# Second product's weights loaded and summed ahead of the last gates, the last gates spread by SyncE's queue, residuals and identity in rooms of their own

## The chip, the cores and the metric

The kernel runs on one core of one Trainium2 chip. The metric is the device time of one execution in microseconds, as a median over runs. The profile is that of one execution, and its times are counted from the start of its span. The engines are TensorE (PE, with its weight loads as PEld), VectorE (DVE), ScalarE (ACT), GpSimd (POOL) and SyncE (SP, which here only issues DMAs).

## What is computed

The input x has 64 sequences of 64 channels of length 1024. A state-space convolution is taken along the length, masked by each sequence's length. Its result, 4096 tokens of 1024 values, goes through a mixture of 64 low-rank experts: scores, the best 16 with softmax gates, one product into rank space, the gates, and one product back. The result is added to x.

```python
def _L0_ffn_ref(x, A, B, Wr):
    ...
    scores = xf @ Wr.T
    top_vals, top_idx = jax.lax.top_k(scores, TOPK)
    gates = jax.nn.softmax(top_vals, axis=-1)
    G = jnp.zeros((N, K), xf.dtype).at[jnp.arange(N)[:, None], top_idx].set(gates)
    h = jnp.einsum('nd,krd->nkr', xf, A)
    out = jnp.einsum('nkr,kdr->nd', h * G[:, :, None], B)
    return (out * SCALING).reshape(*prefix, -1)
x = x + _L0_ffn_ref(_L0_cond_ref(x, itok_B_8_3872, L0_cond_log_dt, L0_cond_C, L0_cond_log_A_real, L0_cond_A_imag, L0_cond_D), L0_ffn_A, L0_ffn_B, L0_ffn_Wr)
```

All of it is in float32. The two einsums are products of 1024 x 1024 weights (A and B with their experts and ranks laid in one row) with the 4096 tokens.

## The kernel before

The channels are taken in eight groups of eight (HG), 512 tokens each. For a group, conv() makes y, gates() makes the scores on PE (psh, psc) and the softmax of the best 16 on DVE (ex), and spread_gates() transposes ex on PE with the identity (pg), stores it to gt_dram from ACT's queue and loads it back with every row repeated for 16 partitions. These eight loads of 256 KB into four gx tiles are issued by POOL (G.dma_start, L694).

Both products use a scheme of seven smaller products in place of eight (Strassen's, in Winograd's form), with sums of weight quarters and of right-hand quarters. In the first product, first() and seven() run it for a group in two halves, j = 0 and j = 2, with the products in the order 1, 6, 2, 7, 5, 4, 3; products 1 and 2 share a PSUM bank (c11), 5 and 3 another (c12). The pool ps_f has four banks. DVE takes the results out of them: u2, u3, c22 (the tile h_p, L317) and two more adds into u3 and u2 (h_u). finish() then multiplies the four quarters by the gates into one tile, hg: DVE the first quarter (b11, L721), straight from the bank c11, and POOL the other three (L715). POOL stores hg[0:3] to hg_dram, DVE makes four sums of the quarters (t1, b12, t2, t4, in sums()), and POOL stores hg[3:7] (L718). The pool hp of hg has one buffer, so each half waits for the stores of the half before it.

Around the groups, the convolution of the next group is woven into the first product of the present one, so that PE has work all the time. At the last group, 7, there is no next convolution.

The second product needs the weights of B: quarters() loads them in eight pieces of 512 KB on SP's queue (L163) into the tiles wb (s3, a22, a11, a12), factors() adds four sums of four pieces each on DVE (add_by_vector, L212), and second_level() makes, for each of the seven products, another four sums (L760), since second() runs the seven-product scheme a second time inside each of them. Their tiles lie in the pool wpb on the right side of the on-chip memory, which is opened after right.close(), that is, over the constants, the x tiles and the tables of the convolution. The constants include the identity and the tile two, both read by gates() and spread_gates().

second() runs 28 rounds, four pairs of groups (sg) by seven products n in the order 1, 6, 7, 2, 5, 4, 3. A round has seven products of its own, 1, 6, 7, 2, 5, 4, 3 again, of eight matmul instructions each in the trace, into banks named s. The right-hand tiles of a round come by SP from hg_dram (r, b_room or qy, 2 x 512 KB, loaded four rounds ahead) and get four sums on DVE (second_sums(), L777). What a round gives is added into acc_a, b_room and the output tiles o, partly on DVE from the banks (L306, L317), partly on POOL from on-chip memory (L799). The o tiles begin as the residual x, loaded by SP in fours (residuals()) into a pool op of twelve tiles, and are stored by SP. The pool op is opened after left.close(), so its tiles lie over gp, tq and hp.

Most instructions are ordered by a scheduler from the order of the program and its own costs; where the code says tc.keep_in_program_order(), an instruction keeps its place among its engine's others. Each engine works off its instructions in order. A DMA waits on the queue of the engine that issues it, and with it whatever that engine issues later.

Of the kernel before, what the change touches and what calls it, by code (L numbers as in the profile page):

```python
# [37 lines left out]
F32 = mybir.dt.float32  # L38
I32 = mybir.dt.int32
AF = mybir.ActivationFunctionType  # L40
ALU = mybir.AluOpType
# [3 lines left out]
P = 128  # L45
# [47 lines left out]
def body(ctx: ExitStack, tc, x, xo, lens, par, dvec, at, bm, wt, cst, out):  # L93
# [7 lines left out]
    def pool(stack, name, bufs, side, **kw):  # L101
        return stack.enter_context(tc.tile_pool(name=name, bufs=bufs, side=side, **kw))
# [9 lines left out]
    fp = pool(ctx, "fp", 2, "left")  # L112
    gp = pool(left, "gp", 1, "left")
    tq = pool(left, "tq", 1, "left")
    const = pool(right, "const", 1, "right")
    xp = pool(right, "xp", 4, "right")
    tp = pool(right, "tp", 1, "right")
# [6 lines left out]

    par_sb = const.tile([P, 5, NP], F32, tag="par", name="par_sb")
    nc.sync.dma_start(par_sb, par)
    cst_sb = const.tile([P, NW + P + 2 + NBLK], F32, tag="cst", name="cst_sb")
    nc.scalar.dma_start(cst_sb, cst)
    lens_sb = prep.tile([P, NB], I32, tag="lens", name="lens_sb")
    d_sb = const.tile([P, NH], F32, tag="dvec", name="d_sb")  # L130
# [3 lines left out]
    ident = cst_sb[:, NW : NW + P]  # L134
    identsel = cst_sb[:, NW : NW + P + 2]
    feat = cst_sb[:, NW + P + 2 :]
    two = const.tile([P, NE], F32, tag="two", name="two")

    krows = dram.tile([NH, KROW], F32, tag="krows", name="krows")

# [539 lines left out]
    def spread_gates(g, ex, spread):  # L680

        pg = ps_k.tile([NE, TOK], F32, tag="pk", name=f"pg_{g}")
        for t in range(NTT):
            tc.keep_in_program_order(nc.tensor.transpose(pg[:, t * P : (t + 1) * P], ex[:, t, :], ident))
        gt = gp.tile([NE, TOK], F32, tag="gt", name=f"gt_{g}")
        nc.scalar.copy(gt, pg)
        nc.scalar.dma_start(gt_dram[g], gt)
        n = P // RANK
        for j in range(0, KH, 2):
            for m in range(2):  # L690
                gx = gxp.tile([P, 2, TOK], F32, tag="gx", name=f"gx_{g}_{j}_{m}")
                for ii in range(2):
                    c = m * KH + j + ii
                    G.dma_start(  # L694
                        gx[:, ii, :],
                        gt_dram[g, c * n : (c + 1) * n, :].unsqueeze(1).to_broadcast([n, RANK, TOK]),
                    )
                spread[m, j] = gx


# [3 lines left out]
    def first(g, y, spread):  # L704

        rf = right_factors(y.rearrange("p k s h b -> p k s (h b)"), f"ty{g}_")

        def finish(j, c11, u2, u3, c12, p4, c22):
            hg = hp.tile([P, 7, 2, HT], F32, tag="hg", name=f"hg_{g}_{j}")

            def gate(m, s):
                return spread[m, j][:, :, s * HT : (s + 1) * HT]

            def gt_(o, a, b, op):
                G.tensor_tensor(out=o, in0=a, in1=b, op=op)  # L715

            def store(a, b):
                nc.gpsimd.dma_start(hg_dram[g, :, a:b, j : j + 2, :], hg[:, a:b])  # L718

            b11, b21, b22, t4, t1, t2, b12 = (hg[:, n] for n in range(7))  # L720
            i = V.tensor_tensor(out=b11, in0=c11, in1=gate(0, 0), op=ALU.mult)  # L721
            if g == 0:
                tc.keep_in_program_order(i)
            gt_(b22, c22, gate(1, 1), ALU.mult)
            tt(u3, p4, u3, ALU.subtract)
            gt_(b21, u3, gate(1, 0), ALU.mult)
            tt(u2, c12, u2, ALU.add)
            gt_(b12, u2, gate(0, 1), ALU.mult)
            store(0, 3)

            def sums():
                tt(t1, b11, b12, ALU.subtract)
                tt(b12, b22, b12, ALU.subtract)
                tt(t2, b22, t1, ALU.add)
                tt(t4, b21, t2, ALU.subtract)
                store(3, 7)

            unsummed.append(sums)

        for j in range(0, KH, 2):  # L740
            for n, _ in enumerate(seven(wa, rf, j, f"h{g}", finish)):
                if n == 1:
                    sum_factors()
                yield
# [3 lines left out]
    def sum_factors():  # L748
        while unsummed:
            unsummed.pop()()  # L750
# [32 lines left out]
    def second(places, rooms, loaded, next_loaded, made, second_level_of, spare, pools):  # L783
# [2 lines left out]

        op, ps, A, B = pools
        todo = [(sg, n) for sg in range(NG // 2) for n in (1, 6, 7, 2, 5, 4, 3)]
        outs = {}

        def residuals(sg, m, s):
            for a in range(2):
                for gg in range(2):
                    o = op.tile([P, 2, HT], F32, tag="o", name=f"o_{sg}_{m}{s}{a}{gg}")
                    queued(o.rearrange("p i t -> p (i t)"), xo[2 * sg + gg, m, s, a])
                    outs[m, s, a, gg] = o

# [96 lines left out]
        for q, (sg, n) in enumerate(todo):  # L894
            if q + 1 < len(todo):
                steps = second_sums(r_of.pop(q + 1), *rooms(q + 1))
            else:
                steps = iter(())

            def ahead_step():  # L900
                next(later, None)
                try:
                    next(steps)
                except StopIteration as e:
                    if e.value is not None:
                        sums[q + 1] = e.value

            right_ = sums.pop(q)
            left_ = made[n]
            early, late = now  # L910
            later = second_level_of(todo[q + 3][1]) if q + 3 < 7 else iter(())

            def product(i, bank=None, more=False):
                first = bank is None
                if first:
                    banks, t = (ps, "ps") if more else (ps_f, "pf")
                    bank = banks.tile([P, 2, HT], F32, tag=t, name=f"s{sg}_{n}_{i}")
                for ii in range(2):
                    for k in range(2):
                        nc.tensor.matmul(  # L920
                            bank[:, ii, :], lhsT=left_[i - 1][:, k, ii * P : (ii + 1) * P],
                            rhs=right_[i - 1][:, k, :],
                            start=(first and ii == 0 and k == 0),
                            stop=(ii == 1 and k == 1 and not more),
                            skip_group_check=True,
                        )
                return bank

            def new(t, i):
                return fp.tile([P, 2, HT], F32, tag=t, name=f"{t}{i}_{sg}_{n}")  # L930

            c11 = product(1, more=True)
            p1 = new("p", 1)
            nc.scalar.copy(p1, c11)  # L934
            p6 = product(6)
            v2 = new("u2", 2)
            tt(v2, p1, p6, ALU.subtract)
            early((0, 1), v2)
            ahead_step()
            p7 = product(7)  # L940
            v3 = new("u3", 3)
            tt(v3, p7, v2, ALU.add)
            early((1, 1), v3)
            early((1, 0), v3)
            product(2, c11)
            if q == 0:
                sum_factors()
            late((0, 0), c11, None)
            ahead_step()
            c12 = product(5, more=True)  # L950
            late((1, 1), c12, v3)
            ahead_step()
            p4 = product(4)
            late((1, 0), p4, v3)
            ahead_step()
            product(3, c12)
            late((0, 1), c12, v2)
            ahead_step()
            if q + 1 < len(todo):
                ahead, *now = parts_of(*todo[q + 1])  # L960
                ahead()
            if n in behind:
                residuals(sg, *behind[n])
            elif n == 4 and sg + 1 < NG // 2:
                residuals(sg + 1, 0, 0)
            if q + 4 < len(todo):
                r_of[q + 4] = places(q + 4)
                load_factor(*todo[q + 4], r_of[q + 4])
# [18 lines left out]
    for g in range(NG):  # L987
        ex = gates(g, y)
        spread = {}
        if products is not None:  # L990
            for _ in steps:
                pass
            if g + 1 == NG:

                ahead(products, 13 - done[0])
                spread_gates(g, ex, spread)
            for _ in products:
                pass
# [16 lines left out]
        for n in conv(g + 1, steps, got):  # L1015
            ahead(products, 1 if n is None else n)
        y = got.pop()
    right.close()
    wpb = pool(ctx, "wpb", 1, "right")
    sums = factors(*(factor(wpb, "wb", t) for t in ("s4", "s2", "s1")),  # L1020
                   *quarters(wpb, bm, "wb", nc.sync), add_by_vector, wb)
    made, spare = {}, {}
    room_of = {7: "a11", 2: "s2", 5: "s1", 4: "a22", 3: "s4"}

# [33 lines left out]
    n = 0  # L1058
    for _ in products:
        n += 1  # L1060
        if 4 <= n <= 9:
            ahead(sums, 3)
        if n == 9:
            es = [second_level_of(i, part(ey, k * NE2, 3, 2, L // 4)) for k, i in enumerate((1, 6))]
            es.append(second_level_of(7))
        if n >= 9:
            ahead(es[(n - 9) // 2], 3)
        if n == 10:
            loaded = tuple(gxp.tile([P, KH, HT], F32, tag="gx", name=f"r0_{gg}") for gg in range(2))
            load_factor(0, 1, loaded)  # L1070
# [13 lines left out]
        return pool(ctx, name, bufs, "left")  # L1084

    tp2 = lpool("tp2", 1)
    op = lpool("op", 12)
    qy = in_y("qy")
    A = four(wp.tile([P, KH, L // 2], F32, tag="a12", name="acc_a").rearrange("p k t -> p (k t)"))

# [51 lines left out]
```

## Time and profile before

| | us |
|---|---|
| median of 3 runs (1021.19 to 1022.26) | 1021.33 |
| the profiled execution | 1021.93 |
| its span, first to last instruction | 1020.2 |
| PE busy | 989.2 |
| PE weight loads busy (beside PE) | 740.6 |
| DVE busy | 718.6 |
| POOL busy | 336.2 |
| ACT busy | 165.9 |

The granted PE clock is 0.992 of full speed over the span. The convolution and the first product fill the span to about 668 us, and the second product the rest. A matmul of 128 x 256 in float32 appears as two instructions. In a line of the timeline the columns are start, duration, engine, line of the kernel, operation, output tile, input tiles, shape, count, and in brackets how long the engine was idle before and what ended it. In a line of the stretches the columns are the stretch, its length, the busy time of PE, PEld, DVE, ACT and POOL with their counts, the granted clock, the DMA share and GB/s.

### The profile page before, as it was taken

Reading aid. Unit: us, or ns where it says so; the run is one execution under the profiler, and the core shown is the slowest. Engines: PE = TensorE matmul, PEld = TensorE weight load, DVE = VectorE, ACT = ScalarE, POOL = GpSimd, SP = SyncE. Lnnn points to the kernel's source line nnn. Section 1 sums busy time; section 2 is a strip of 40 time slices with the busy share of each in tenths; the row PEclk is TensorE's granted clock in tenths of the full one; section 3 lists DMA queues with packets and bytes.
Section 4 is the critical chain, followed back from the end, with each engine's and each line's share of the span. In section 5 each row is a group of like instructions: output and inputs, shape, how many; then the busy total and the mean of one; then the engine's idle time right before and its main releaser. Section 6 shows DMA issues by size and latency. Waiting matters only on the chain.

```text
span 1020.2 us, 12148 instructions
## 1 busy us (share of the span) xinstructions
PE 989.2 (97%) x4416; PEld 740.6 (73%) x4416; DVE 718.6 (70%) x1672; ACT 165.9 (16%) x339; POOL 336.2 (33%) x286
## 2 busy tenths in 40 slices
PE   7999999999999999999999996998999999999998
PEld 2466656686686686686686585886888888888887
DVE  6887788587586587577567552988975785686674
ACT  5435041131131131131101000000000000000000
POOL 0012023023023023122122131226663764555565
PEclk9999999999999999999999998998999999999999
DMA  7213316316315315315314128455466268357432
GB/s 268 64 59 118 107 51 188 131 40 152 135 49 150 134 52 150 135 51 150 135 53 129 73 90 235 155 195 187 152 222 225 80 213 285 93 202 261 127 122 103
DMA packets 66253, 140.87 MB, mean 138 GB/s; under 512 B 9938, under 2 KB 18450, under 8 KB 66194
## 3 DMA queue, kind: packets, MB, share of 16 engines
q1 hardware_dynamic: 48288, 92.44, 27.0%
q0 software_dynamic: 16896, 46.18, 14.8%
q10 hardware_dynamic: 1010, 1.48, 0.6%
q8 instruction: 35, 0.57, 0.2%
q14 instruction: 24, 0.20, 0.1%
HBM read 92.79 MB, written 47.25 MB: 137 GB/s over the span
## 4 chain that ended last, share of the span: by engine, by line
PE 88%; DVE 5%; DMA 4%; issue 2%; POOL 0%; SPq 0%; ACT 0%; DVEq 0%; POOLq 0%; ACTq 0%
PE h L501 33%; PE s L920 31%; PE pc L580 6%; PE pc L586 5%; PE pu L554 5%; PE psh L639 3%; PE sum L189 2%; DMA hg_dram<-hg 2%; DMA gx<-gt_dram 1%; DVE t L777 1%; PE pb L276 1%; DMA waa<-in_at 1%; PE psc L648 1%; PE pb L278 1%; DVE e L760 1%
## 5 line engine op out<-in xcount | busy, mean ns | idle before, releaser
L317 DVE SCALAR_TENSOR_TENSOR s<-s,turn 128x64 f32<-128x64 f32 (+1 forms) x576 | 146.0, 302 | 36.7 <-ACT s L559 30.2
L501 PE MATMUL h<-y,was 128*128 128x256 f32 x512 | 119.7, 386 | 10.7 <-DVE h_p L317 10.7
L501 PE MATMUL h<-y,waa 128*128 128x256 f32 x512 | 122.7, 384 | 0.0
L501 PEld LDWEIGHTS h<-y,was 128*128 128x128 f32 x512 | 97.3, 193 | 31.5 <-DVE h_p L317 11.1
L501 PE MATMUL h<-ty,was 128*128 128x256 f32 x512 | 116.4, 380 | 0.0
L501 PEld LDWEIGHTS h<-y,waa 128*128 128x128 f32 x512 | 93.7, 190 | 27.0 <-issue 15.4
L501 PEld LDWEIGHTS h<-ty,was 128*128 128x128 f32 x512 | 96.6, 190 | 16.7 <-issue 3.9
L715 POOL TENSOR_TENSOR hg<-h_p,gx 128x512 f32<-128x512 f32 x16 | 27.3, 1706 | 227.0 <-DVE h_p L317 223.7
L715 POOL TENSOR_TENSOR hg<-h_u,gx 128x512 f32<-128x512 f32 x32 | 49.2, 1537 | 134.3 <-DVE h_u L306 134.1
L694 POOL DMA_DIRECT2D gx<-gt_dram x64 | 38.4, 624 | 101.9 <-DMA gt_dram<-gt 92.2
L934 ACT COPY p<-s 128x512 f32<-128x512 f32 x28 | 16.4, 587 | 321.5 <-PE s L920 299.6
L592 DVE TENSOR_TENSOR y<-pc,mask 128x512 f32<-128x512 f32 x64 | 42.4, 684 | 37.0 <-PE pc L586 37.0
L799 POOL TENSOR_TENSOR o<-o,acc_a 128x512 f32<-128x512 f32 x32 | 48.7, 1540 | 50.1 <-ACT acc_a L817 21.5
L580 PE MATMUL pc<-x,toep 128*128 128x512 f32 x128 | 62.0, 607 | 0.0
L306 DVE TENSOR_TENSOR hg<-hg 128x512 f32<-128x512 f32 x64 | 42.8, 688 | 26.9 <-POOL hg L715 26.0
L501 PE MATMUL h<-ty,waa 128*128 128x256 f32 x256 | 58.8, 382 | 0.0
L559 ACT COPY s<-pu 128x448 f32<-128x448 f32 x64 | 34.0, 532 | 140.8 <-PE pu L554 140.4
L586 PE MATMUL pc<-s,w 64*128 64x448 f32 x256 | 56.8, 562 | 0.0
L501 PEld LDWEIGHTS h<-ty,waa 128*128 128x128 f32 x256 | 47.9, 190 | 10.7 <-issue 4.6
L554 PE MATMUL pu<-x,bt 128*64 128x448 f32 x256 | 55.5, 553 | 0.0
L799 POOL TENSOR_TENSOR o<-o,b_room 128x512 f32<-128x512 f32 x32 | 50.0, 1581 | 9.8 <-DVE b_room L306 9.8
L306 DVE TENSOR_TENSOR o<-o,s 128x512 f32<-128x512 f32 x52 | 35.4, 681 | 23.6 <-PE s L920 17.9
(225 smaller groups left out, 1632.7 us busy)
## 6 DMA issues: line engine op xcount, KB each, us to landing
x<-in_x SPq DMA_DIRECT2D x32, 512.0 KB, 5.4
gx<-gt_dram POOLq DMA_DIRECT2D x64, 256.0 KB, 6.8
hg_dram<-hg POOLq DMA_DIRECT2D x16, 1024.0 KB, 6.0
o<-in_xo SPq DMA_DIRECT2D x64, 256.0 KB, 4.5
out<-o SPq DMA_DIRECT2D x64, 256.0 KB, 2.0
qy<-hg_dram SPq DMA_DIRECT2D x28, 512.0 KB, 3.6
r<-hg_dram SPq DMA_DIRECT2D x26, 512.0 KB, 6.6
hg_dram<-hg POOLq DMA_DIRECT2D x16, 768.0 KB, 4.4
```

The lines of the kernel that those rows point to most:

```text
L306: V.tensor_tensor(out=o, in0=a, in1=b, op=o_)
L317: V.scalar_tensor_tensor(out=o, in0=a, scalar=s, in1=b, op0=o1, op1=o2)
L501: nc.tensor.matmul(bank[:, ii, :], lhsT=fac[n - 1][:, k, (j + ii) * P : (j + ii + 1) * P], rhs=rf[n - 1][:, k, :], start=(first and ii == ...
L554: nc.tensor.matmul(pu[hh * NS : (hh + 1) * NS, :], lhsT=bt[:, i, (1 - c) * P + hh * NS : (1 - c) * P + (hh + 1) * NS], rhs=xt[:, hh, : NCH ...
L559: nc.scalar.copy(s[:, c], pu.rearrange("p (k b) -> p k b", b=NB))
L580: nc.tensor.matmul(pc, lhsT=toep[:, 2 * i + hh, :], rhs=xt[:, hh, :], start=True, stop=False)
L586: nc.tensor.matmul(pcs[hh][:, NB:], lhsT=w[o : o + NS, c, i, 1:], rhs=s[o : o + NS, c].rearrange("p k b -> p (k b)"), start=False, stop=(c ...
L592: marks["y"] = V.tensor_tensor(out=y[:, :, :, 2 * i + hh, :], in0=pcs[hh].rearrange("p (k s b) -> p k s b", s=NS2, b=HB), in1=mask.rearran ...
L694: G.dma_start(gx[:, ii, :], gt_dram[g, c * n : (c + 1) * n, :].unsqueeze(1).to_broadcast([n, RANK, TOK]),)
L715: G.tensor_tensor(out=o, in0=a, in1=b, op=op)
L799: tc.keep_in_program_order(G.tensor_tensor(out=o, in0=a, in1=b, op=op_))
L920: nc.tensor.matmul(bank[:, ii, :], lhsT=left_[i - 1][:, k, ii * P : (ii + 1) * P], rhs=right_[i - 1][:, k, :], start=(first and ii == 0 an ...
```

## The change

Four things are done. The identity and the tile two get a pool of their own (ids), so that the rest of the right side can be closed without waiting for the last gate transposes; the pool wpb is opened, and the weight quarters are loaded, before the last group's gates are spread. The last group's gates are loaded by SP's queue in place of POOL's, in program order. In the last group the first gate multiply (b11) is put behind the three that POOL makes, and kept there; the sums of the weights and the second-level sums are asked for earlier among the last group's products, with one more second-level set (n = 2) before the second product begins. The residuals get three pools of four tiles in place of one of twelve, and in the first round of second() the waiting sums of hg are made ahead of product 2.

```diff
@@ body
+    ids = pool(ctx, "ids", 1, "right")
     const = pool(right, "const", 1, "right")
...
-    cst_sb = const.tile([P, NW + P + 2 + NBLK], F32, tag="cst", name="cst_sb")
+    cst_sb = ids.tile([P, NW + P + 2 + NBLK], F32, tag="cst", name="cst_sb")
...
-    two = const.tile([P, NE], F32, tag="two", name="two")
+    two = ids.tile([P, NE], F32, tag="two", name="two")
@@ spread_gates
+        queue = nc.sync if g + 1 == NG else G
...
-                    G.dma_start(
+                    i = queue.dma_start(
                         gx[:, ii, :],
                         gt_dram[g, c * n : (c + 1) * n, :].unsqueeze(1).to_broadcast([n, RANK, TOK]),
                     )
+                    if queue is nc.sync:
+                        tc.keep_in_program_order(i)
@@ first / finish
-            i = V.tensor_tensor(out=b11, in0=c11, in1=gate(0, 0), op=ALU.mult)
-            if g == 0:
-                tc.keep_in_program_order(i)
+            def first_quarter():
+                i = V.tensor_tensor(out=b11, in0=c11, in1=gate(0, 0), op=ALU.mult)
+                if g in (0, NG - 1):
+                    tc.keep_in_program_order(i)
+
+            last_group = g + 1 == NG
+            if not last_group:
+                first_quarter()
             gt_(b22, c22, gate(1, 1), ALU.mult)
             tt(u3, p4, u3, ALU.subtract)
             gt_(b21, u3, gate(1, 0), ALU.mult)
             tt(u2, c12, u2, ALU.add)
             gt_(b12, u2, gate(0, 1), ALU.mult)
+            if last_group:
+                first_quarter()
             store(0, 3)
@@ second
-        outs = {}
+        outs, loads = {}, [0]
 
         def residuals(sg, m, s):
+            room = op[loads[0] % len(op)]
+            loads[0] += 1
...
-                    o = op.tile([P, 2, HT], F32, tag="o", name=f"o_{sg}_{m}{s}{a}{gg}")
+                    o = room.tile([P, 2, HT], F32, tag="o", name=f"o_{sg}_{m}{s}{a}{gg}")
...
-            product(2, c11)
             if q == 0:
                 sum_factors()
+            product(2, c11)
@@ body, the last group
             if g + 1 == NG:
-
+                right.close()
+                wpb = pool(ctx, "wpb", 1, "right")
+                wb_quarters = quarters(wpb, bm, "wb", nc.sync)
                 ahead(products, 13 - done[0])
                 spread_gates(g, ex, spread)
...
-    right.close()
-    wpb = pool(ctx, "wpb", 1, "right")
     sums = factors(*(factor(wpb, "wb", t) for t in ("s4", "s2", "s1")),
-                   *quarters(wpb, bm, "wb", nc.sync), add_by_vector, wb)
+                   *wb_quarters, add_by_vector, wb)
...
-        if 4 <= n <= 9:
-            ahead(sums, 3)
-        if n == 9:
-            es = [second_level_of(i, part(ey, k * NE2, 3, 2, L // 4)) for k, i in enumerate((1, 6))]
-            es.append(second_level_of(7))
-        if n >= 9:
-            ahead(es[(n - 9) // 2], 3)
+        if n <= 4:
+            ahead(sums, 5)
+        if n in (5, 6):
+            i = (1, 6)[n - 5]
+            ahead(second_level_of(i, part(ey, (n - 5) * NE2, 3, 2, L // 4)), 5)
+        if n in (9, 11):
+            ahead(second_level_of((7, 2)[(n - 9) // 2]), 5)
...
-    op = lpool("op", 12)
+    op = [lpool(f"op{i}", 4) for i in range(3)]
```

## The prediction, made before the changed kernel ran

> **What bounds the kernel now.** I read the page's forty slices first, then who TensorE (PE) waited for, then the timeline around each wait, then the stretches.
>
> ```profile
> PE   7999999999999999999999996998999999999998
> ...
> PEclk9999999999999999999999998998999999999999
> ```
>
> PE is busy almost everywhere; the chain of waits gives it 88% of the span. Two places are open: near 612 to 637 us and near 688 to 714 us. So only what closes PE's gaps there counts. The waits name them (engine and line, what it waited for, total us, times, longest):
>
> ```profile
> PE h L501 <- DVE h_p L317: 10.7, 1, 10.7
> PE s L920 <- DVE acc_a L306: 4.3, 1, 4.3
> PE s L920 <- DVE acc_a L317: 1.8, 1, 1.8
> ```
>
> The first is one wait in group 7, the last group of the first product. Its timeline (start, us, engine, line, what; idle before):
>
> ```profile
> 603.43 0.37 SPq L163 DMA_DIRECT2D wbs<-in_bm  x1
> ...
> 609.58 3.62 POOL L694 DMA_DIRECT2D gx<-gt_dram x6 [1.02 <-DMA gt_dram<-gt]
> ...
> 621.02 0.81 POOL L718 DMA_DIRECT2D hg_dram<-hg  x1 [2.13 <-DMA gx<-gt_dram]
> 623.64 3.43 PEld L501 LDWEIGHTS h<-ty,waa 128*128 128x128 f32 x16
> 623.85 3.62 PE L501 MATMUL h<-ty,waa 128*128 128x256 f32 x16
> 634.42 0.69 DVE L721 TENSOR_TENSOR hg<-h,gx 128x512 f32<-128x512 f32 x1 [16.67 <-DMA hg_dram<-hg]
> ...
> 637.43 0.68 DVE L317 SCALAR_TENSOR_TENSOR h_p<-h_u,h 128x512 f32<-128x512 f32 x1
> ...
> 638.16 2.07 PE L501 MATMUL h<-y,was 128*128 128x256 f32 x4 [10.69 <-DVE h_p L317]
> ```
>
> The hg tile has one buffer. VectorE (DVE) stands in order at the first gate multiply of group 7 (L721) until group 6's store of that tile has landed; h_p, for which PE waits, is four adds behind it. The store was issued at 621.02 and landed 13.2 us later (other stores: median 5.6). It was late twice over: POOL issued it behind eight gate loads, and it then shared the DMA engines with them and with the 4.2 MB of weights. The stretches show that load piled up while the time before it was empty (last columns: PE clock, DMA share, GB/s):
>
> ```profile
> 595.00:600.00 5.00, 5.00 (x25) 4.41 (x24) 2.81 (x8) 0.42 (x1) 0.00 (x0) 1.00 0.00 0
> ...
> 606.00:610.00 4.00, 4.00 (x20) 3.54 (x19) 1.03 (x2) 0.00 (x0) 2.68 (x3) 1.00 1.00 348
> ...
> 625.00:630.00 5.00, 2.47 (x12) 1.83 (x10) 0.00 (x0) 0.00 (x0) 0.00 (x0) 1.00 1.05 224
> ```
>
> The second place is different: DVE itself is full (11.38 of 12 us between 692 and 704).
>
> ```profile
> 701.07 3.78 PE L920 MATMUL s<-b_room,ey 128*128 128x256 f32 x8 [4.34 <-DVE acc_a L306]
> ...
> 704.64 3.85 PE L920 MATMUL s<-qy,wbs 128*128 128x256 f32 x12
> ```
>
> **What PE loses.** A product of the second stage, eight matmuls, starts every 1.73 us (0.2155 each); sixteen of the first take 3.45. First place: 10.69 idle, and the sixteen after it take 638.16 to 643.60, 5.44, so 1.99 of slow clock: 12.7. Second place: 1.76; 4.34, then 701.07 to 708.33 for twenty matmuls, 7.26 against 4.31, so 2.95; 0.24 at 724: 9.3. Cross-check: 28 rounds of 7 products are 28 x 12.1 = 339, and PE runs from 667.8 to 1016.2, 348.4. So 22.0 can be had at most.
>
> **What the Trainium skill says.** "TensorE: Matmul & The Clock Gate", Part 1, has the clock halve after an idle window of about 3.4 us and recover after such a window of work. The trace agrees: 10.7 and 4.3 us idle are followed by 1.99 and 2.95 lost, the 1.8 us idle by nothing. "SBUF — State Buffer", Who interferes with whom: a DVE instruction with two SBUF inputs and a GpSimd one that reads SBUF exclude each other. Here an SBUF add takes 0.68 alone and 1.75 beside POOL, while adds with a PSUM input stay at 0.68. "DMA: Bandwidth & Descriptors", Queues, rings and completion order: the engines take packets from the queues in turn, so a small store suffers from another queue's backlog; the 13.2 us agree.
>
> **The change, part by part.** The order of the built instructions tells what the diff leaves open: PE's order is the same but for three matmuls late on, ACT's is the same, and POOL loses the eight gate issues.
>
> *Weights earlier.* With identity and two elsewhere, the first weight load waits for group 7's score matmuls (psh, last at 588.8) instead of the gate transposes (pg, 603.3). So 4.2 MB start at 588.9. The same eight loads at the kernel's start ran at 260 to 400 GB/s; about 13 us, done near 602, in the empty stretch. They sit on SP's queue, with nothing urgent behind. Cost nothing.
>
> *Gates by SP.* The gate store to DRAM is still issued at 604.0, now on an empty DMA, and lands in 2.2 us (the quickest landing in that tile's view) to 5.3 (this one). SP then issues eight loads at about 0.42 each; the last pair waits for POOL's last multiply of group 6 (about 610.5). POOL saves 8 x 0.62. Gates (2.1 MB) and group 6's two stores (1.8 MB, the second issued near 614 instead of 621) at the 230 to 350 GB/s seen here take 11 to 17 us from 607: landed 618 to 624. SP's next loads (r, first right-hand factor) wait for the gate buffers anyway.
>
> *DVE's order.* Group 7's first gate multiply now stands behind the last add of its half, and the 16 weight sums stand ahead and between. From ty at 606.3: 23 instructions before h_p at a pitch of 0.61 are 14.0, plus 0.5 for POOL and 2 blocked adds at 1.1: 623. h_p's bank is full at 624.0, so h_p ends at 624.8; PE reaches its reader at 627.5. Margin 2.7. The first stall goes, with its clock: 12.7, and PE enters the second stage at 655.1 instead of 667.8. What is late next: second-half banks need h_u at 628.6 (used 634.7), the c12 add at about 633 (642), the gate multiply at about 634 (645.5), its h_p at 649.8 (652.5). r is issued near 630 and 634 and is wanted at 650; b_room is issued at 645.5, 3.6 us to land, wanted at 653. No wait is left there that I can find. If gates or store are late by up to 7 us more, only POOL's multiplies slip, which PE feels first through a bank at 649.
>
> *Second stage.* Here the same 22 SBUF adds and 16 PSUM adds remain between the first round's last release and the fourth's; before, they took 41.4 us (682.8 to 724.2) and PE wants them in 34. What improves: group 7's sums, weight tails and the n=2 set are off DVE before it (the 1.8 stall goes: the acc_a it waited for is computed 1 us ahead of need); and the first residuals, in a room of their own, no longer wait for the last hg store: issued at about 658 behind qy rather than 683.9, 2 us after PE's first round ended. 3.1 MB of qy and residuals against 1.8 MB of stores land at 664 to 670, so POOL starts its four adds before the second round, not 4.6 us into it. Walking DVE from 667.9: 13 instructions to the acc_a that frees c12 in round two, 13 x 0.61 = 7.9, plus 2 to 6 blocked adds at 1.1, gives 678.1 to 682.4; PE arrives at 678.9 (three matmuls of the next product are now ahead). Stall 0 to 3.5; I take 2.3. Over 3.4 the clock would cost up to 2.95 more; I take 0.7. Later rounds: 0 to 1.5, take 0.5. Loss left 3.5 of 9.3, bounds 0 and 9.3.
>
> *Residual pools.* Three times four tiles instead of twelve in one: the loads turned round in fours already. Apart from the early start nothing.
>
> **Sum.** The profiled execution took 1021.93: span 1020.2 and 1.7 around it; its median runs are 0.6 below it. Saving 12.7 + 9.3 - 3.5 = 18.5: span 1001.7, profiled 1003.4, median 1021.33 - 18.5 = 1002.8.
>
> **Rivals.** (a) The second stage keeps its loss: DVE plus POOL are the bound there, the same instructions in the same 41 us. For it: DVE at 12.00 of 12 from 716 to 728. Against: residuals are earlier and three sets of adds are gone. 1021.33 - 12.7 = 1008.6. (b) A new wait takes part of the first stall: gates or group 6's store land near 634 again, so POOL and the gate multiply (which frees PE's bank for 645.5) slip. For: 2 KB gate pieces ran at only 200 to 260 GB/s after 620. Against: the weights are out of the way. Half the stall back, 6 us: 1009 to 1012. (c) Slower: DVE's adds blocked by POOL's multiplies. 32 weight adds stand in 606 to 651; at 1.1 each that is 35 us if all collide, less some 13 us of free DVE time, 22, and the second stage's 9.3 stays: 999.3 + 22 + 9.3 = 1031. It loses against before only from (22.0 - 9.3 + 13) / 1.1, about 24 blocked adds; POOL has nine multiplies there. (d) It does not do what it says, the loads are held by something else: 1021. The order's waits speak against it.
>
> **How the numbers follow.** Forecast 0.60 (1002.8, own range 999.3 to 1006.5); (a) 0.24; (b) 0.10; (c) 0.04; (d) 0.02. Floor 1021.33 - 22.0 = 999.3; a little below it for scatter, and up through (a) and the better part of (b): 998.5 to 1011. A measurement here tells 0.2%, 2 us, from none. Faster: forecast, (a), (b), 0.94; same 0.02; slower 0.04.
>
> **What would show it.** Weight loads from 589 and an empty DMA by 603; no PE wait on h_p; group 6's last store landed before 625; the second stage's first matmul near 655; POOL's first residual add before 670; a PE wait of 0 to 3.5 us on acc_a near 680. Wrong if PE waits in the second half of group 7, if r or qy is late, or if acc_a's wait is again over 4 us with a slow clock behind it.

## The result, and the profile after

| | before | after |
|---|---|---|
| median, us | 1021.64 (1021.19 to 1022.26, 4 runs) | 1004.26 (1003.97 to 1005.58, 4 runs) |
| profiled execution | 1021.93 | 1004.42 |
| its span | 1020.2 | 1002.6 |
| granted PE clock | 0.992 | 0.998 |

The ratio is 0.9832, with a 95% interval from 0.9815 to 0.9849: 17.4 us less. Of the 17.6 us by which the profiled span is shorter, 0.6 were won ahead of group 7 (the scores of the last group start at 584.55 in place of 585.16, which another run of the same kernel does not repeat: 585.36).

The page of the kernel after, its forty slices: of the two open places one 8 is left, and no slice has a clock below 9.

```profile
PE   7999999999999999999999999998999999999998
...
PEclk9999999999999999999999999999999999999999
```

Who PE waited for longest after 560 us (engine and line, what it waited for, total us, times, longest). There is no wait on h_p any more; acc_a is left.

```profile
PE s L933 <- DVE acc_a L307: 3.2, 1, 3.2
PE s L933 <- DVE o L307: 0.4, 1, 0.4
```

The timeline of the kernel after at the first place (start, duration, engine, line, what; in brackets the idle time before it and what ended it):

```profile
588.35 0.37 SPq L164 DMA_DIRECT2D wbs<-in_bm  x1
...
605.74 6.43 SPq L696 DMA_DIRECT2D gx<-gt_dram  x8
...
614.44 0.81 POOL L722 DMA_DIRECT2D hg_dram<-hg  x1 [3.50 <-DVE hg L307]
...
623.44 0.69 DVE L318 SCALAR_TENSOR_TENSOR h_p<-h_u,h 128x512 f32<-128x512 f32 x1 [1.48 <-PE h L502]
...
626.69 3.62 PE L502 MATMUL h<-y,was 128*128 128x256 f32 x16
```

The weights are asked for at 588.35 instead of 603.43, group 6's second store goes out at 614.44 instead of 621.02, and h_p is done at 624.13, 2.6 us before PE comes to it. In the stretches of the same kernel (stretch, its length, busy times of PE, PEld, DVE, ACT and POOL, clock, DMA share, GB/s) the weights fill what was empty, and after 622 nothing is left to carry:

```profile
590.00:595.00 5.00, 5.00 (x25) 4.41 (x25) 4.34 (x29) 0.42 (x1) 0.00 (x0) 1.00 1.00 354
595.00:600.00 5.00, 5.00 (x25) 4.41 (x24) 3.29 (x8) 0.00 (x0) 0.39 (x1) 1.00 1.03 383
...
622.00:628.00 6.00, 6.00 (x30) 5.28 (x29) 4.49 (x6) 0.00 (x0) 1.63 (x1) 1.00 0.08 31
```

The second place, in the timeline of the kernel after:

```profile
656.30 15.67 SPq L776 DMA_DIRECT2D o<-in_xo  x8
...
670.51 4.61 POOL L812 TENSOR_TENSOR o<-o,acc_a 128x512 f32<-128x512 f32 x3 [3.38 <-DMA o<-in_xo]
...
675.20 5.05 POOL L812 TENSOR_TENSOR acc_a<-acc_a,u 128x512 f32<-128x512 f32 x3
...
675.72 1.75 DVE L788 TENSOR_TENSOR t<-qy 128x512 f32<-128x512 f32 x1
677.50 1.64 DVE L788 TENSOR_TENSOR t<-qy,t 128x512 f32<-128x512 f32 x1
679.06 1.74 DVE L788 TENSOR_TENSOR qy<-qy 128x512 f32<-128x512 f32 x1
680.73 0.67 DVE L307 TENSOR_TENSOR acc_a<-acc_a,s 128x512 f32<-128x512 f32 x1
...
681.46 3.46 PE L933 MATMUL s<-b_room,ey 128*128 128x256 f32 x8 [3.23 <-DVE acc_a L307]
684.71 0.86 PE L933 MATMUL s<-qy,wbs 128*128 128x256 f32 x2
```

Read it backwards. PE waits 3.23 us for an add into acc_a. Ahead of that add DVE works off three sums for a later round, each with two inputs in on-chip memory, each stretched from 0.68 to about 1.7 us beside POOL. POOL is busy there with acc_a's own adds, because its four adds into the first residuals came before them, and three of those waited until 670.51 for a load. The ten matmuls after the wait take 681.46 to 685.40, the start of the next row of PE: 3.94 us against 10 x 0.2155, so 1.8 of slow clock. The loss left is 3.23 + 1.8 + 0.45 (the wait on o) = 5.5 us.

The same chain in the kernel before:

```profile
690.20 4.66 POOL L799 TENSOR_TENSOR o<-o,acc_a 128x512 f32<-128x512 f32 x3 [2.17 <-DMA o<-in_xo]
...
700.34 0.67 DVE L306 TENSOR_TENSOR acc_a<-acc_a,s 128x512 f32<-128x512 f32 x1
```

Counted from the start of the second stage (667.77 before, 654.32 after), POOL's last three adds into the residuals came 6.2 us earlier (16.2 instead of 22.4) and the add that PE waits for 6.2 us earlier (26.4 instead of 32.6).

One profiled execution below (e4, one pool) lasted 2956 us, with first-product matmuls of about 949 ns where a second run of that kernel (e4b) has 384, and is not read.

### The profile page after: what moved, and what is told of

Same layout as the page of the kernel before. It is cut to its first block, busy times and chain, and to the rows that moved or that the text cites. A ratio compares the mean times of both kernels' runs of the same rounds, so it can differ in the third digit from the quotient of the medians.

```text
span 1002.6 us, 12158 instructions
## 1 busy us (share of the span) xinstructions
PE 985.1 (98%) x4416; PEld 738.4 (74%) x4416; DVE 717.5 (72%) x1672; ACT 165.8 (17%) x339; POOL 330.8 (33%) x278
## 3 DMA queue, kind: packets, MB, share of 16 engines
q10 hardware_dynamic: 1010, 1.48, 0.6%
## 4 chain that ended last, share of the span: by engine, by line
PE 96%; DVE 3%; DMA 1%; issue 0%; SPq 0%; DVEq 0%
PE h L502 38%; PE s L933 33%; PE pc L581 6%; PE pc L587 5%; PE pu L555 5%; PE psh L640 3%; PE sum L190 2%; PE pb L277 1%; DMA waa<-in_at 1%; PE psc L649 1%; PE pb L279 1%; DVE t L788 0%; DVE y L593 0%; PE pg L685 0%; PE pk L292 0%
## 5 line engine op out<-in xcount | busy, mean ns | idle before, releaser
L696 POOL DMA_DIRECT2D gx<-gt_dram x56 | 33.5, 625 | 97.2 <-DMA gt_dram<-gt 90.3
```

What stands on the lines that cost most here:

```text
L696: i = queue.dma_start(gx[:, ii, :], gt_dram[g, c * n : (c + 1) * n, :].unsqueeze(1).to_broadcast([n, RANK, TOK]),)
```

## The experiments

Three questions were open: which part of the change removes the first stall, what the rooms for the residuals are worth, and what holds acc_a in the second stage.

**The order alone, on the kernel before (e1).**

```diff
-            i = V.tensor_tensor(out=b11, in0=c11, in1=gate(0, 0), op=ALU.mult)
...
+            if last_group:
+                first_quarter()
             store(0, 3)
```

> The kernel before with one edit: the last group's first gate multiply (the one that needs h_u) is issued behind the gate multiplies of c22, u3 and u2. Weights, gate loads, residual rooms and identity stay as in the kernel before. Theory (the order on VectorE, with h_u waiting for the store of group 6, is what made TensorE wait for h_p): TensorE's wait on h_p of 10.7 us goes with 2.0 us of slowed clock, although group 6's second store still lands near 634 us; the stall at the start of the second stage stays at 9.3 us or grows to 12, as its data come as late as before; median 1009 to 1012 us. Rival (the late store itself holds the last group, through crowded DMA engines): the wait on h_p stays and the median is 1019 to 1022 us.

Measured: 1012.0 us (1009.49 to 1015.06), ratio 0.9909 [0.9885, 0.9933]. Its longest PE waits after 560 us:

```profile
PE s L927 <- DVE acc_a L306: 3.5, 1, 3.5
PE s L927 <- DVE acc_a L317: 2.5, 1, 2.5
PE h L501 <- DVE h_p L317: 2.0, 1, 2.0
```

and two lines of its timeline:

```profile
635.71 0.69 DVE L722 TENSOR_TENSOR hg<-h,gx 128x512 f32<-128x512 f32 x1 [5.16 <-DMA hg_dram<-hg]
...
652.55 5.41 PE L501 MATMUL h<-y,was 128*128 128x256 f32 x16 [2.02 <-DVE h_p L317]
```

The store still holds DVE until 635.71, but only what stands behind it there; PE runs on to 650.5 and then waits 2.0 us, for the h_p of the second half. The second stage starts at 657.80 instead of 667.77; 1.1 us of this were won ahead of group 7 (its scores start at 584.06 instead of 585.16), and the order is worth the other 8.9 of the 12.7. So the long wait was one of order on DVE, as the theory had it; that 2.0 us of it come back half a group later, with 1.8 of slow clock, it had not. The second stage waits 3.5 and 2.5 us, against 4.3 and 1.8.

**The change without the new order (e2).**

```diff
-            last_group = g + 1 == NG
+            last_group = False
```

> The changed kernel with the last group's first gate multiply back at its old place, ahead of the gate multiplies of c22, u3 and u2; everything else stays changed. Theory (each of the two repairs is enough alone: weights loaded earlier let group 6's second store land near 621.5 us, and h_u is then ready by about 620.6 us): TensorE waits under 1 us on h_p; median 1003.5 to 1005.5 us. Rival (only the new order takes the wait away): TensorE waits 5 to 10 us on h_p and the median is 1010 to 1015 us.

Measured: 1003.04 us (1002.25 to 1004.07), ratio 0.9821 [0.9805, 0.9837]. PE's longest wait after 560 us:

```profile
PE s L933 <- DVE acc_a L307: 2.7, 1, 2.7
```

Its timeline at the first place:

```profile
624.00 0.69 DVE L726 TENSOR_TENSOR hg<-h,gx 128x512 f32<-128x512 f32 x1 [2.48 <-issue]
...
625.80 0.68 DVE L318 SCALAR_TENSOR_TENSOR h_p<-h_u,h 128x512 f32<-128x512 f32 x1
...
627.45 3.62 PE L502 MATMUL h<-y,was 128*128 128x256 f32 x16
```

The gate multiply is again ahead and starts only at 624.00, and h_p is done at 626.48, 1.0 us before PE (627.45). The margin has shrunk from 2.6 to 1.0, and nothing is lost. The rest of the change takes the whole stall without the new order; beside it the order is a second lock on the same door. Which share of this belongs to the early weights and which to the gate loads on SP's queue, this run doesn't separate.

**The weights late again (e5b).** The identity and the tile two go back into the pool of the constants (not shown in the cut), and the weights are asked for behind the gate loads; the rest of the change is kept.

```diff
...
-                right.close()
-                wpb = pool(ctx, "wpb", 1, "right")
-                wb_quarters = quarters(wpb, bm, "wb", nc.sync)
                 ahead(products, 13 - done[0])
                 spread_gates(g, ex, spread)
+                right.close()
+                wpb = pool(ctx, "wpb", 1, "right")
+                wb_quarters = quarters(wpb, bm, "wb", nc.sync)
```

> The changed kernel with the second product's weights issued behind the last group's gate loads instead of ahead of them; identity and the constant two are back in the pool of the constants. New order of VectorE and of the gate multiplies, and the rooms for the residuals, stay. Theory (the early issue of the weights, before the gates are known, is what leaves the DMA engines free for gates and stores): the weights land near 615 to 626 us, VectorE is held at its sums of weights in front of the last gates, and TensorE waits 3 to 10 us; median 1007 to 1014 us. Rival (the last product of the conv is long enough to cover the loads wherever they stand): 1003.5 to 1005.5 us.

Measured: 1019.98 us (1017.0 to 1025.17), ratio 0.9994 [0.9977, 1.0011]. From its timeline:

```profile
614.14 0.41 SPq L163 DMA_DIRECT2D wbs<-in_bm  x1
615.48 9.80 SPq L163 DMA_DIRECT2D wba<-in_bm  x5
...
631.24 1.29 DVE L212 TENSOR_TENSOR wbs<-wbs,wba 128x512 f32<-128x512 f32 x2 [17.26 <-DMA wba<-in_bm]
...
640.08 1.22 PE L501 MATMUL h<-y,waa 128*128 128x256 f32 x2 [13.08 <-DVE h_u L306]
```

Six of the eight loads were issued behind the gate loads, DVE stood 17.26 us at a sum of weights, and the h_u for which PE waited was queued behind it. The direction was expected, the size was not (a wait of 13.1 us against 3 to 10, 1019.98 us against 1007 to 1014). With its sums asked for early, the change depends on its early loads: without them nearly everything is given back. But this is another wait than that of the kernel before. Group 6's second store (1024 KB, from the list of DMA issues between 605 and 640: count, size, us to landing) was on time here:

```profile
hg_dram<-hg POOLq DMA_DIRECT2D x1, 1024.0 KB, 8.9
```

It went out at 613.54, so it had landed by 622.4, where the one of the kernel before, behind POOL's gate loads, went out at 621.02 and took 13.2 us. So this run shows what the early sums need, not that the early weights are what brings the store in. No run has the gate loads back on POOL's queue, or on SP's alone; what each of the two parts is worth for the first stall stays open.

**One pool for the output tiles (e4, e4b).**

```diff
-    op = [lpool(f"op{i}", 4) for i in range(3)]
+    op = [lpool("op", 12)]
```

> The changed kernel with the second product's output buffers in one pool of 12 again in place of three pools of 4, so that the first residual loads wait for the last of the gated products' stores instead of an earlier read. Theory (when the residuals land sets GpSimd's first add, which decides with VectorE when the accumulators come free): the first residuals land 3 to 6 us later, TensorE's first wait grows from 3.2 to 5 to 7 us, median 1006 to 1009 us. Rival (VectorE's own list of sums is what TensorE waits for, and the rooms are worth nothing): no change, 1003.5 to 1005 us.

> The same kernel as in the run with one pool of 12 output buffers, for a profile at the speed of the others. From its timed executions of 1006.1 to 1007.6 us: TensorE's wait on the first accumulator is 5 to 6 us in place of 3.2, and the first residuals land 3 to 6 us later. Rival (the difference is only the chip's own scatter): the wait is 3.2 us and the median 1004 us.

Measured: 1006.42, 1007.63 and 1006.14 us in the timed executions of the first, 1006.18 us (1004.87 to 1006.98) in the second, ratio 0.9838 [0.9822, 0.9855]. From the timeline of the second:

```profile
668.25 3.66 SPq L776 DMA_DIRECT2D o<-in_xo  x8
...
674.37 4.61 POOL L812 TENSOR_TENSOR o<-o,acc_a 128x512 f32<-128x512 f32 x3 [1.63 <-DMA o<-in_xo]
...
683.08 3.78 PE L933 MATMUL s<-b_room,ey 128*128 128x256 f32 x8 [4.66 <-DVE acc_a L307]
```

The loads are issued at 668.25 instead of 656.30, POOL's last three adds start 3.9 us later (674.37 against 670.51), and PE waits 4.66 us in place of 3.23. That is less than the 5 to 6 us expected, with the median in the range. The rooms are worth about 2 us. Twelve microseconds of earlier issue bought four to five of earlier adds: in the kernel after the residuals stood behind the loads of qy.

**Sums for later rounds kept back (e6): the fourth factor's (e6_pin3), then the third's too (e6_pin23).**

```diff
-                steps = second_sums(r_of.pop(q + 1), *rooms(q + 1))
+                steps = second_sums(r_of.pop(q + 1), *rooms(q + 1), pinned=q + 1 == 3)
```

> The changed kernel with the sums of the fourth right-hand factor kept in program order on VectorE, so that its three additions of two SBUF operands no longer stand ahead of the accumulation that TensorE's first factor of the second stage waits for. Theory (additions for later rounds, each stretched to 1.75 us beside GpSimd, are what remains of the stall): TensorE's wait of 3.2 us falls to under 1 us and the slowed clock of 1.8 us with it; median 998.5 to 1001 us. Rival (VectorE is full for the rounds that follow, so the same additions hold TensorE there): the wait comes back in a later round, at 2 to 4 us; median 1003 to 1006 us.

> As the run before, with the third right-hand factor's sums kept in program order too. Theory (additions for later rounds are what remains of the stall): 998.5 to 1001 us. Rival (they hold TensorE later instead): 1003 to 1006 us, with a wait on a factor's sum in round three in place of the wait on the accumulator.

Measured: 1003.54 us (1002.26 to 1005.24), ratio 0.9815 [0.9796, 0.9834], and 1004.92 us (1003.26 to 1006.02), ratio 0.9826 [0.9807, 0.9844]. PE's longest waits in the first after 560 us, and one line of its timeline:

```profile
PE s L933 <- DVE o L307: 2.2, 1, 2.2
PE s L933 <- DVE b_room L307: 1.0, 1, 1.0
PE s L933 <- DVE acc_a L307: 0.7, 1, 0.7
...
677.19 0.69 DVE L307 TENSOR_TENSOR acc_a<-acc_a,s 128x512 f32<-128x512 f32 x1 [2.38 <-POOL acc_a L812]
```

The wait on acc_a shrank as asked, and 3.2 us of others came in its place; in sum 3.9 against 3.7 (4.8 in the second run). The theory's 998.5 to 1001 us was missed and its rival came, the wait in a later round. With the three sums out of the way, DVE stood idle for 2.38 us until POOL had done its own add into acc_a, and the sums kept back met POOL's next adds from 683.83 on, at about 1.75 us each. So a new order on DVE alone only moved the loss.

**POOL's four adds left out (e7).** The output then lacks that product.

```diff
-                return (all_of(out_(0, 0), A, ALU.add),) + into(A, -1)
+                return ((nothing if sg == 0 else all_of(out_(0, 0), A, ALU.add)),) + into(A, -1)
```

> The changed kernel without GpSimd's four additions of the first accumulator into the first residuals (so the output's first quarter of token groups 0 and 1 lacks that product). Theory (GpSimd's additions beside VectorE's are what stretches these, and what keeps the accumulator): TensorE's wait of 3.2 us falls to under 1 us; median 998.5 to 1001.5 us. Rival (VectorE's own number of additions sets it, with or without GpSimd): 1003 to 1005 us.

Measured: 998.66 us (998.25 to 999.39), ratio 0.9768 [0.975, 0.9785]. After 655 us PE waits once, for 0.4 us. So without these four adds in POOL's queue all of the loss goes but this. The scheduler also moved the fourth factor's three sums on DVE behind the add that PE waits for, so this run points to POOL's adds but doesn't prove that they alone matter.

**The residuals in front of the right-hand factors (e8), the same with the old place of the gate multiply (e9)**, with the kernel after beside them on the same chip.

```diff
+        residuals(0, 0, 0)
         for q in (2, 3):
             r_of[q] = places(q)
             load_factor(*todo[q], r_of[q])
-        residuals(0, 0, 0)
```

> The changed kernel itself once more, beside the two runs that follow, on the same chip: 1003.5 to 1005 us, with TensorE's wait on the first accumulator at 3.2 us.

> The changed kernel with the four first residual loads issued ahead of the four loads of the third and fourth right-hand factors on SyncE's queue, instead of behind them. Theory (GpSimd's four additions into the first residuals wait for loads that stand behind 2 MB of factors, and so hold the accumulator): they land before 664 us instead of 665.9 and 670.5, GpSimd's additions to the accumulator start near 670 instead of 675.2, TensorE's wait of 3.2 us and its slowed clock go; median 998.5 to 1000.5 us. Rival (the factors then come late, or the sums of a later round take the stall over): 1002 to 1006 us.

> As the run before, and the last group's first gate multiply at its old place too. If the new place only costs (the run with the old place was 1.2 us below the changed kernel, with a wait of 2.7 in place of 3.2 us and no slowed clock behind it): 998 to 1000 us, at or up to 1 us below the run before. Rival (that difference was the shorter wait's alone): equal to the run before within 0.5 us.

Measured: 1004.51 us (1004.33 to 1005.07) for the kernel after, 1003.24 us (1000.58 to 1003.96), ratio 0.9817 [0.9794, 0.984], with the residuals in front, and 1002.28 us (999.8 to 1004.33), ratio 0.9816 [0.9792, 0.984], with the old place of the gate multiply too. From the timeline of the second:

```profile
663.18 2.51 POOL L812 TENSOR_TENSOR o<-o,acc_a 128x512 f32<-128x512 f32 x2
...
671.82 1.76 DVE L788 TENSOR_TENSOR ey<-qy 128x512 f32<-128x512 f32 x1
...
679.38 3.54 PE L933 MATMUL s<-b_room,ey 128*128 128x256 f32 x8 [1.97 <-DVE acc_a L307]
```

POOL's adds now start with acc_a itself, at 663.18, in time that DVE spends waiting for PE. But the scheduler took the third factor for late and moved its sums from 667.21 to 671.82, into POOL's next adds. PE waits 1.97 us and 1.8 of slow clock follow. The forecast of 998.5 to 1000.5 us was missed, and its rival came: the sums of a later round took the stall over. The last two kernels can't be told apart (their runs overlap), so the new order neither helps nor measurably hurts.

**The residuals between the two factors (e10).**

```diff
             load_factor(*todo[q], r_of[q])
-        residuals(0, 0, 0)
+            if q == 2:
+                residuals(0, 0, 0)
```

> The changed kernel with the four first residual loads issued behind the third right-hand factor's two loads and ahead of the fourth's two. VectorE's order then keeps the third factor's three sums where they stood, early, and the fourth's three move behind the accumulations of round two. Theory (GpSimd's additions wait for residuals behind 2 MB of factors, and the third factor's sums must not move into GpSimd's busy time, as they did with the residuals in front): the residuals land by 664 us, TensorE's wait on the first accumulator is under 0.7 us, no slowed clock follows; median 998.5 to 1000.5 us. Rival (VectorE is the bound of the first rounds wherever the sums stand): the waits of all rounds add up to 3 to 4 us again; 1001 to 1004.5 us.

Measured: 999.57 us (999.14 to 999.85), ratio 0.9783 [0.9769, 0.9796]: the best of all that compute the whole, 4.7 and 4.9 us below the two runs of the kernel after, which ran beside other runs of the kernel before (1021.84 us here, 1021.64 and 1021.32 there). PE's waits after 560 us:

```profile
PE s L934 <- DVE o L307: 0.4, 1, 0.4
PE psh L640 <- DVE y L593: 0.3, 1, 0.3
```

From its timeline:

```profile
655.98 2.17 SPq L776 DMA_DIRECT2D o<-in_xo  x4
...
663.34 2.51 POOL L812 TENSOR_TENSOR o<-o,acc_a 128x512 f32<-128x512 f32 x2
...
667.84 0.68 DVE L788 TENSOR_TENSOR ey<-qy 128x512 f32<-128x512 f32 x1
...
674.40 2.95 POOL L812 TENSOR_TENSOR acc_a<-acc_a,u 128x512 f32<-128x512 f32 x2 [1.23 <-DVE u L307]
...
676.14 0.67 DVE L307 TENSOR_TENSOR acc_a<-acc_a,s 128x512 f32<-128x512 f32 x1
...
677.39 1.89 PE L934 MATMUL s<-b_room,ey 128*128 128x256 f32 x8
...
677.82 0.68 DVE L788 TENSOR_TENSOR t<-qy 128x512 f32<-128x512 f32 x1
```

The same adds are done by the same engines. POOL is through with the residuals by 669.7, its adds into acc_a end at 677.35 instead of 680.25, and the add that PE needs runs at 676.14 instead of 680.73. The residuals are issued less than 1 us earlier than in the kernel after (655.98 against 656.30, in a run that started 0.6 later); what changed on SP's queue is that two loads of 512 KB, not four, stand ahead of them.

A second thing changed with it, as was expected: the scheduler moved the fourth factor's three sums behind the add that PE needs (the first is at 677.82, and each takes 0.68 us, as POOL has done its adds), where the kernel after has them ahead of it. Much the same place for these sums, with the residuals late, left 3.9 us of waits (e6_pin3); residuals earlier still, but with the third factor's sums in POOL's time, left a stall of 1.97 and 1.8 of slow clock (e8). So neither DVE's order nor the early residuals was enough by itself; what e10's place of the residuals is worth with DVE's old order no run shows.

## Why the prediction was right, and where it was off

- **The weights early: right.** Predicted issued from 588.9 and in by about 602; measured 588.35, and 383 GB/s until 600. With the sums asked for early, the change needs it (e5b); that it alone takes the first stall is not shown.
- **Gates, stores and h_p: right.** Predicted landed between 618 and 624 with a margin of 2.7 us at h_p; measured an idle DMA after 622 and a margin of 2.6.
- **The first stall and its clock go, 12.7 us: right.** The second stage starts 13.45 us earlier, 12.8 without the 0.6 of the start. That two repairs were made for one stall the prediction did not say: the order alone takes 8.9 us of it (e1), the rest of the change without the order all of it (e2), and the two together no more.
- **A new wait in group 7 (rival b), DVE blocked by POOL's multiplies (rival c), no effect (rival d): none came.**
- **The second stage keeps its loss (rival a): partly.** 5.5 of 9.3 us are left, where the forecast had 3.5.
- **The term that was mis-sized is the loss left in the second stage.** The stall was taken as 2.3 and was 3.2, inside the 0 to 3.5 worked out; DVE's add came at 680.73, inside the 678.1 to 682.4. The slow clock was taken as 0.7, with a loss only above 3.4 us of stall, and was 1.8 after a stall of 3.23; this condition was wrong. The later rounds were taken as 0.5 and were 0.45. Together 2.0 us too little, of which 1.5 are left in the median.
- **What the prediction missed in that step:** it saw the residuals land at 664 to 670 behind qy and called it early enough, since POOL "starts its four adds before the second round". One of the four did (665.87 against 666.41); the other three waited for their loads until 670.51, 4.1 us into the round. e10 beside e6_pin3 shows that this decides, and e8 that DVE's order does too: POOL's adds into the residuals fall either into DVE's idle time or onto DVE's adds. Its floor of 999.3 us was sound: e10, with no stall left but 0.4, has 999.57.

## What to carry to other kernels

Loads whose room can be freed earlier belong into the stretch where the DMA engines are empty; that leaves the DMA engines to the later transfers, and (here together with the gate loads on another queue) may make a second repair of the same stall needless. When two engines that slow each other share an accumulation, look for the idle time of one in which the other's work fits, and order the loads so that it can start there; moving the adds about within the full stretch only moves the wait. After moving a load, look again at what the scheduler made of the other engines' order.

## What the hardware showed unexpectedly

**After a stall of 2 to 2.7 us the clock cost 1.8 us or next to nothing, and the length did not decide which.** The cost beyond the wait itself, counted as above from the matmuls that follow:

| kernel | PE idle, us | lost to the clock, us |
|---|---|---|
| before | 10.69, 4.34 | 1.99, 2.95 |
| one pool (e4b) | 4.66 | 2.75 |
| after, after again | 3.23, 3.12 | 1.8, 1.8 |
| without the new order (e2) | 2.67 | 0.1 |
| order alone (e1) | 2.02, 2.47, 3.46 | 1.8, 1.8, 1.8 |
| residuals in front (e8, e9) | 1.97, 1.97 | 1.8, 1.8 |
| later sums kept back (e6_pin3, e6_pin23) | 2.20, 2.19 | 0.1, 0.1 |
| weights late, second stage (e5b) | 2.53 | 0.1 |
| before | 1.76 | 0.1 |

Between 1.97 and 2.67 us both outcomes stand side by side. The granted clock agrees (third figure from the right, first in the kernel after behind 3.23 us of stall, then in e2 behind 2.67):

```profile
681.00:685.40 4.40, 3.94 (x10) 3.15 (x11) 3.25 (x6) 0.00 (x0) 0.00 (x0) 0.61 0.38 153
...
681.00:684.00 3.00, 2.35 (x11) 2.10 (x12) 3.00 (x6) 0.00 (x0) 0.00 (x0) 1.00 0.92 368
```

The executions of e8 fall into two sets: four with a mean clock of 0.998 took 1003.06 to 1003.96 us, two with 1.0 took 1000.58 and 1001.77. The Trainium skill, "TensorE: Matmul & The Clock Gate", Part 1, asks for an idle window of about 3.4 us before the clock is halved; the losses after 1.97 to 3.23 us of idle time don't fit that, and the measurement decides. The same part says that the window is free-running, of 3413 ns; by estimate from this figure, a window at half clock loses 1.7 us, near the 1.8 measured. The position of the stall against the window may decide, but no run here shows the windows. For reading results it means that a kernel with a stall of some 2 us can differ by about 2 us from one execution to the next.

**POOL is slowed by DVE too.** The Trainium skill, "SBUF — State Buffer", Who interferes with whom, has a DVE instruction with two inputs in on-chip memory and a POOL instruction that reads it contend for one shared pair of ports. DVE's side is above (0.68 us and about 1.7), and the trace agrees for POOL's: POOL's four adds into the residuals took a median of 1.27 us with the residuals in front (e8), where DVE mostly waited, and 1.48 in the kernel after (up to 1.71).
